# A four-layer graph network on one core: how layer 1's node stage begins

## The chip, the cores and the metric

The kernel runs on one core of one Trainium2 chip. The metric is the device time of one execution, in microseconds. The five engines of the core are called TensorE (PE in the profile; its weight loads are PEld), VectorE (DVE), ScalarE (ACT), GpSimd (POOL) and SyncE (SP); each has an instruction queue of its own and works through it in order. SyncE is used only to issue DMA transfers.

## The reference

There are 4096 nodes with 512 features in `x`, and 65536 edges. Four layers each compute `x = x + layer(relu(layernorm(x)))`. What matters here is the end of layer 0 and the beginning of layer 1:

- Layer 0 is an attention over the graph with 8 heads of 64 features. For each node and head it sums weighted rows of the neighbours, divides by the sum of the weights of that head, puts the heads side by side to a row of 512, and takes a softmax over the 512 values. `x1 = x + softmax(row)`.
- Layer 1 is a graph convolution. With `h = relu(layernorm(x1))` and `d = 1/sqrt(degree)`, a node's result is `relu(d * sum over neighbours of (d * h) @ weight)`. The kernel applies the weight first: `y = d * (h @ weight)` for all nodes, and then sums rows of `y` along the edges.
- Layer 2 (messages by a small network on each edge) and layer 3 (again a convolution) follow; nothing of them is touched.

## The kernel before

The 4096 nodes are 32 blocks of 128, one node per partition. `acc` is a tile in SBUF with one row of 522 values per node: 512 sums, 8 sums of weights (one for each head), and the node's degree. It lives through the whole kernel.

Layer 0's node part and its sorting of edges come first. Then layer 0's loop (`attend`, called through `in_two` at L816) runs over 544 tiles of 128 edges in groups of 8: GpSimd issues indirect DMAs that gather rows of `htab` (L453), ScalarE and VectorE make the weights, TensorE multiplies with one-hot matrices (L761), and VectorE adds the sums to `acc` (L768). In this loop SyncE issues nothing. The order of its instructions is written out by hand (`manual_schedule`).

Then comes the stage that this document is about, the beginning of layer 1 (L857 to L887). Here no order is written out: the framework's planner orders the instructions of each engine by its own estimate of when their inputs are ready, with the program's order as priority, so that instructions of later blocks stand between those of earlier ones. The stage works as follows.

- It loads the weight `w_sb` (1 MB) through `load_w` (L432), makes `dis`, the `1/sqrt(degree)` of all nodes, with `rsqrt` (L396 to L401: a logarithm and an exponential on ScalarE, then one Newton step of four VectorE instructions), and `rden`, the reciprocals of all the sums of weights (L862).
- It then takes the blocks in eight groups of four (`BG = 4`). For a group it loads four blocks of `x` (L865, 1 MB) into `xt`, which has two buffers.
- For each block of the group: multiply the 512 sums by the 8 reciprocals, each spread over its 64 features (L870, VectorE); row maximum (L872); its negative (L873); exponential with the row's sum (L875, ScalarE); reciprocal of that sum (L876); multiply and add to `xt` (L877).
- The group's `xt` is stored to `x1` (L878). `Norm` then makes mean and variance of each of its rows (L390, L391) and the reciprocal standard deviations of all four blocks together: add epsilon (L413) and `rsqrt`.
- For each block again: normalize into `hn` (L418), transpose it on TensorE (L425, four 128x128 pieces), ReLU into SBUF on ScalarE (L427), multiply with `w_sb` (L442; eight TensorE instructions for a block), scale by `dis` on ScalarE (L886), and store to `ytab` in HBM (L887).

Layer 1's loop over the edges (`sum_edges`) gathers rows of `ytab` by indirect DMAs on GpSimd's queue (L453), so its first gather needs all 32 blocks of `ytab`.

Two more places are named in the prediction. L448 makes one-hot matrices on VectorE; one of layer 1's loop is placed early, between instructions of this stage. And the end of layer 2 has additions on GpSimd (L1266 and L1287, 128x1024 values each) while VectorE computes norms (L1227 to L1239) and scales rows (L1303, L1305).

Of the kernel before, what the change touches and what calls it, by code (L numbers as in the profile page):

```python
# [10 lines left out]
F32 = mybir.dt.float32  # L11
# [6 lines left out]
PSUM = bass.MemoryType.PSUM  # L18
DRAM = bass.MemoryType.DRAM

P = 128
# [13 lines left out]
def kernel(  # L35
# [23 lines left out]
    nc = tc.nc  # L59
    N, D = x.shape  # L60
    E, DE = edge_attr.shape
    H, _, F = w0.shape
    KC = D // P
    NB = N // P
# [52 lines left out]
    x1 = dram.tile([N, D], F32, name="x1")  # L117
# [227 lines left out]
    class Side:  # L345


        def __init__(self, *work):
            self.work = list(work)
# [38 lines left out]
    def stats(pool, st, ap):  # L388
        six = pool.tile([P, 6], F32, name="six")
        nc.vector.bn_stats(six, ap)  # L390
        nc.vector.bn_aggr(st, six)  # L391

    def rsqrt(pool, o, ap, n):

        root = pool.tile([P, n], F32, name="root")
        nc.scalar.activation(root, ap, AF.Ln)  # L396
        nc.scalar.activation(o, root, AF.Exp, scale=-0.5)
        nc.vector.tensor_mul(root, o, o)
        nc.vector.tensor_mul(root, root, ap)
        nc.vector.tensor_scalar(root, root, -0.5, 1.5, op0=OP.mult, op1=OP.add)  # L400
        nc.vector.tensor_mul(o, o, root)  # L401

    BG = 4

    class Norm:


        def __init__(self, pool, rows):
            self.st = pool.tile([P, BG, 2], F32, name="st")
            for j, ap in enumerate(rows):  # L410
                stats(pool, self.st[:, j, :], ap)
            var = self.st[:, :, 1]
            nc.vector.tensor_scalar(var, var, EPS, None, op0=OP.add)  # L413
            self.rstd = pool.tile([P, BG], F32, name="rstd")
            rsqrt(pool, self.rstd, var, BG)

        def rows(self, j, o, ap):
            nc.vector.tensor_scalar(o, ap, self.st[:, j, 0:1], self.rstd[:, j:j + 1],  # L418
# [2 lines left out]
    def relu_t(pool, ppool, hn, relu=True):  # L421

        ps = ppool.tile([P, KC, P], F32, name="tr")
        for k in range(KC):
            nc.tensor.transpose(ps[:, k, :], hn[:, k * P:(k + 1) * P], ident)  # L425
        h_t = pool.tile([P, KC, P], F32, name="h_t")
        nc.scalar.activation(h_t, ps, AF.Relu if relu else AF.Copy)  # L427
        return h_t

    def load_w(pool, name, ap):  # L430
        t = pool.tile([P, ap.shape[0] // P, D], F32, name=name)
        nc.sync.dma_start(t, ap.rearrange("(k p) d -> p k d", p=P))  # L432
        return t
# [6 lines left out]
    def product(ps, h_t, w_sb, k0=0, start=True, stop=True):  # L440
        for k in range(KC):
            nc.tensor.matmul(ps, h_t[:, k, :], w_sb[:, k0 + k, :],  # L442
                             start=start and k == 0, stop=stop and k == KC - 1)
# [21 lines left out]
    def in_two(o, main, total, run):  # L465

        run(0, main)
        with tc.If(nc.values_load(more[:, o:o + 1], min_val=0, max_val=1) > 0):
            run(main, total)

    def blocks_of(ap, b, n=BG):
        return ap[b * P:(b + n) * P].rearrange("(b p) d -> p b d", p=P)
# [340 lines left out]

    one2 = node_pool.tile([P, 2], F32, name="one2")
    nc.vector.memset(one2, 1.0)
    in_two(0, TS_MAIN, TS, attend)  # L816
    l0_pool.close()

# [35 lines left out]
        return run  # L854

    ytab = dram.tile([N, D], F32, name="ytab")
    with tc.tile_pool(name="l1_w", bufs=1) as wp, tc.tile_pool(name="l1", bufs=2) as lp, \  # L857
            tc.tile_pool(name="l1_ps", bufs=2, space=PSUM) as lps:
        w_sb = load_w(wp, "w_sb", w_l1)
        rsqrt(lp, dis, acc[:, :, D + H], NB)  # L860
        rden = wp.tile([P, NB, H], F32, name="rden")
        nc.vector.reciprocal(rden, acc[:, :, D:D + H])  # L862
        for b0 in range(0, NB, BG):
            xt = lp.tile([P, BG, D], F32, name="xt")
            nc.sync.dma_start(xt, blocks_of(x, b0))  # L865
            for j in range(BG):
                b = b0 + j
                row = acc[:, b, :D]
                o = row.rearrange("p (h f) -> p h f", h=H)
                nc.vector.tensor_mul(o, o, rden[:, b, :].unsqueeze(2).to_broadcast([P, H, F]))  # L870
                top = lp.tile([P, 1], F32, name="top")
                nc.vector.reduce_max(top, row, axis=AX.X)  # L872
                nc.vector.tensor_scalar(top, top, -1.0, None, op0=OP.mult)  # L873
                whole = lp.tile([P, 1], F32, name="whole")
                nc.scalar.activation(row, row, AF.Exp, bias=top, accum_out=whole)  # L875
                nc.vector.reciprocal(whole, whole)  # L876
                nc.vector.scalar_tensor_tensor(xt[:, j, :], row, whole, xt[:, j, :], op0=OP.mult, op1=OP.add)  # L877
            nc.sync.dma_start(blocks_of(x1, b0), xt)  # L878
            norm = Norm(lp, [xt[:, j, :] for j in range(BG)])
            for j in range(BG):  # L880
                b = b0 + j
                hn = lp.tile([P, D], F32, name="hn")
                norm.rows(j, hn, xt[:, j, :])
                ps = lps.tile([P, D], F32, name="y_ps")
                product(ps, relu_t(lp, lps, hn), w_sb)
                nc.scalar.activation(acc[:, b, :D], ps, AF.Copy, scale=dis[:, b:b + 1])  # L886
                nc.sync.dma_start(ytab[b * P:(b + 1) * P, :], acc[:, b, :D])  # L887
# [132 lines left out]
    with ExitStack() as l2:  # L1020
        l2.enter_context(ahead)
        wp = l2.enter_context(tc.tile_pool(name="l2_w", bufs=1))
# [170 lines left out]
    with ExitStack() as end:  # L1193
        R = 2
        own = dict(reuse_waits="tile")
        wp = end.enter_context(tc.tile_pool(name="l2_end_w", bufs=1, **own))
        lp = end.enter_context(tc.tile_pool(name="l2_end", bufs=2, **own))
        lps = end.enter_context(tc.tile_pool(name="l2_end_ps", bufs=2, space=PSUM, **own))
# [60 lines left out]
        for p in range(groups + 4):  # L1259
# [22 lines left out]
            if now(p - 2):  # L1282
                b0 = (p - 2) * R
# [12 lines left out]
            if now(p - 2):  # L1296
                b0 = (p - 2) * R
                y = acc[:, b0:b0 + R, :D]
                xt = xs.pop(p - 2)
                norm = Norm2(y)  # L1300
# [8 lines left out]
                norm = Norm2(xt)  # L1309
# [3 lines left out]
            if now(p - 4):  # L1313
                b0 = (p - 4) * R
# [94 lines left out]
```

## Time and profile before

| | |
|---|---|
| median of 2 timed runs | 5975.68 us (5975.33 to 5976.02) |
| profiled execution, its own time | 6542.29 us |
| profiled execution, span from first to last instruction | 6540.2 us |
| mean granted TensorE clock, profiled | 0.926 |
| last sum of layer 0's loop (L768) | begins 1269.0 us, lasts 0.70 |
| first transpose of this stage (L425) | 1291.9 us |
| last scaling of this stage (L886) | begins 1433.1 us, lasts 0.69 |
| first gather of layer 1's loop (L453) | 1437.5 us |

The profiled execution is longer than the timed ones, so a sum of durations from it is set against its own time.

A line of the timeline gives the start in us, the duration in us (for several merged instructions from the first's start to the last's end), the engine, the line of the kernel, the operation, output `<-` inputs, the shape, how many instructions are merged, and in brackets the idle time of the engine before it and what ended that. "Issue" there means that the engine waited for nothing that the profile shows. A line of the stage table gives, for one stretch of time, the busy time and the number of instructions of each engine, the granted TensorE clock, the mean busy share of the 16 DMA engines, and the GB/s they moved. L-numbers are lines of the kernel before.

### The profile page before, as it was taken

The page shows a single profiled execution, that of the slowest core. Times are in us where ns is not written, and L with a number is a line of the kernel's source. Part 1 is how long each engine was busy: PE and PEld are TensorE (multiplying, and loading weights), DVE is VectorE, ACT ScalarE, POOL GpSimd, SP SyncE. Part 2 cuts the span into 40 slices and gives each one's busy share as a digit, 9 for nine tenths or more (in the row PEclk, how much of TensorE's full clock was granted, in tenths as well). Part 3 has the DMA queues.
Part 4 walks back from the last instruction along what each step waited for, and adds up shares of the span by engine and source line. Part 5 has one row for each costly group of instructions (what it writes and reads, how often), then busy time and mean ns, then how long its engine had stood idle before and what let it go on. Part 6 is the DMA issues. An engine that isn't in the chain of part 4 may idle for free. (4 is left out here: it accounts for less than half of the span.)

```text
span 6540.2 us, 65028 instructions
## 1 busy us (share of the span) xinstructions
PE 5567.4 (85%) x17918; PEld 2951.3 (45%) x17918; DVE 4364.9 (67%) x7420; ACT 3086.2 (47%) x4232; POOL 3919.6 (60%) x3326
## 2 busy tenths in 40 slices
PE   6576777688998869999999999999999899777777
PEld 4355555533443334444444444444444566422222
DVE  7466666755665448888888888888888555455555
ACT  3144444431110047777777777777777433100000
POOL 1255555316665658888888888888887111255664
PEclk9788888899999989999999999999999999877878
DMA  8655555456777745555555555555555111355665
GB/s 228 160 151 149 146 152 153 131 179 211 226 226 197 214 106 115 108 108 108 108 110 109 107 107 108 108 108 109 110 108 104 68 68 65 111 163 165 194 197 161
DMA packets 424659, 908.43 MB, mean 139 GB/s; under 512 B 135734, under 2 KB 135734, under 8 KB 424278
## 3 DMA queue, kind: packets, MB, share of 16 engines
q0 software_dynamic: 264768, 721.66, 44.6%
q1 hardware_dynamic: 159510, 182.40, 8.7%
q8 instruction: 153, 2.51, 0.2%
q14 instruction: 228, 1.87, 0.1%
HBM read 800.88 MB, written 102.94 MB: 138 GB/s over the span
## 5 line engine op out<-in xcount | busy, mean ns | idle before, releaser
L442 PE MATMUL m_ps<-w_sb,h_t 128*128 128x512 f32 x4224 | 1894.1, 596 | 3.2 <-ACT h_t L1081 3.0
L847 PE MATMUL sum_ps<-g,oh 128*128 128x512 f32 x2144 | 1152.5, 673 | 286.5 <-DVE acc L463 145.6
L442 PEld LDWEIGHTS m_ps<-w_sb,h_t 128*128 128x128 f32 x4224 | 781.9, 190 | 937.8 <-issue 922.9
L463 DVE TENSOR_TENSOR acc<-acc,sum_ps 128x512 f32 x800 | 550.0, 687 | 796.7 <-PE sum_ps L847 336.2
L1048 POOL DMA_INDIRECT pg<-qtab,eg x528 | 947.1, 1794 | 161.2 <-issue 160.6
L453 POOL DMA_INDIRECT pg<-ptab,eg x528 | 773.8, 1466 | 217.3 <-issue 160.3
L761 PE MATMUL sum_ps<-rows,oh 128*128 128x261 f32 x2176 | 619.3, 440 | 287.5 <-issue 197.6
L847 PEld LDWEIGHTS sum_ps<-g,oh 128*128 128x128 f32 x2144 | 429.1, 212 | 951.4 <-issue 574.1
L453 POOL DMA_INDIRECT g<-ytab,s_dst x544 | 544.7, 1001 | 491.3 <-DMA x_mid<-x 201.0
L453 POOL DMA_INDIRECT rows<-htab,s_dst x544 | 518.1, 952 | 482.1 <-PE sum_ps L761 285.6
L453 POOL DMA_INDIRECT g<-ztab,d_src x528 | 511.6, 969 | 409.5 <-PE sum_ps L847 173.2
L761 PEld LDWEIGHTS sum_ps<-rows,oh 128*128 128x128 f32 x2176 | 453.5, 217 | 391.8 <-issue 203.8
L988 POOL DMA_INDIRECT eg<-aug,d_eid x528 | 517.6, 980 | 160.9 <-issue 142.9
L1081 ACT COPY h_t<-tr_ps 128x512 f32<-128x512 f32 x528 | 296.3, 587 | 292.5 <-PE tr_ps L1079 271.7
L1349 ACT ACTIVATE t_end<-acc,dis 128x512 f32<-128x512 f32 x32 | 23.0, 722 | 847.9 <-DVE acc L463 806.4
L463 DVE TENSOR_TENSOR acc<-acc,small_ps 128x512 f32 x528 | 362.5, 687 | 80.2 <-DVE acc L463 60.6
L1099 PE MATMUL small_ps<-parts,oh 128*128 128x512 f32 x1056 | 314.9, 420 | 91.4 <-DVE parts L1093 80.7
L1156 DVE TENSOR_TENSOR pg<-pg,small_ps 128x512 f32<-128x512 f32 x528 | 328.3, 683 | 66.3 <-issue 38.6
L1152 DVE TENSOR_TENSOR z<-m_ps,b_bc 128x512 f32<-128x512 f32 x132 | 91.3, 692 | 376.7 <-PE m_ps L442 345.8
L1093 DVE TENSOR_TENSOR parts<-z,parts 128x1024 fp32r<-128x1024 f32 x264 | 323.4, 1225 | 9.0
L1079 PE MATMUL tr_ps<-ident,pg 128*128 128x128 f32 x2112 | 302.3, 276 | 5.4 <-DVE pg L1167 2.1
L768 DVE TENSOR_TENSOR acc<-acc,sum_ps 128x522 f32 x272 | 189.5, 697 | 173.7 <-PE sum_ps L761 159.6
(276 smaller groups left out, 8716.9 us busy)
## 6 DMA issues: line engine op xcount, KB each, us to landing
aug<-row SPq DMA_DIRECT2D x32, 560.0 KB
xt<-in_x_dram SPq DMA_DIRECT2D x16, 1024.0 KB
row<-in_edge_attr_dram SPq DMA_DIRECT2D x32, 512.0 KB
rows<-htab,s_dst POOLq DMA_INDIRECT x544
g<-ytab,s_dst POOLq DMA_INDIRECT x544
eg<-aug,d_eid POOLq DMA_INDIRECT x528
pg<-ptab,eg POOLq DMA_INDIRECT x528
pg<-qtab,eg POOLq DMA_INDIRECT x528
```

Of the source, the lines that this page charges most:

```text
L442: nc.tensor.matmul(ps, h_t[:, k, :], w_sb[:, k0 + k, :], start=start and k == 0, stop=stop and k == KC - 1)
L453: nc.gpsimd.indirect_dma_start(out=dst_ap, out_offset=None, in_=table, in_offset=bass.IndirectOffsetOnAxis(ap=idx, axis=0))
L463: nc.vector.tensor_add(into, into, ps)
L761: nc.tensor.matmul(ps[:, c, :HW], oh[:, j + k, :], rows[:, j + k, c * HW:(c + 1) * HW], start=k == 0, stop=k == 1)
L847: nc.tensor.matmul(ps, oh[:, j + k, :], g[:, j + k, :], start=k == 0, stop=k == pair - 1)
L988: nc.gpsimd.indirect_dma_start(out=eg[:, j // 2, (j % 2) * HALF:(j % 2 + 1) * HALF], out_offset=None, in_=aug.rearrange("e c -> (e c)").un ...
L1048: nc.gpsimd.indirect_dma_start(out=pg[:, j, :], out_offset=None, in_=qtab, in_offset=bass.IndirectOffsetOnAxis(ap=end_of(eg, j, 1), axis=0 ...
L1079: nc.tensor.transpose(h_ps[:, k, :], h[:, j, k * P:(k + 1) * P], ident)
L1081: nc.scalar.copy(h_t, h_ps)
L1093: nc.vector.tensor_sub(parts[:, 1], m, parts[:, 0].bitcast(F32))
L1099: nc.tensor.matmul(ps, oh, parts[:, k], start=k == 0, stop=k == 1)
L1156: nc.vector.tensor_add(nxt[:, j], nxt[:, j], made[j])
```

## The change

The change has four parts.

1. `w_sb` and the first four blocks of `x` (`x_first`, 1 MB) are fetched ahead of layer 0's loop, into a pool `l1_first` on the other side of SBUF that stays open until the stage ends.
2. The first four blocks are worked on in groups of 1, 1 and 2, out of `x_first`; from block 4 on the groups are of four as before. `Norm` and `rsqrt` take the number of blocks of the group.
3. `xt` has three buffers instead of two.
4. The products of the sums with the reciprocals (L870) stay on VectorE for blocks 0 and 1, and are made by GpSimd for blocks 2 to 31.

```diff
     def rsqrt(pool, o, ap, n):
-        root = pool.tile([P, n], F32, name="root")
+        root = pool.tile([P, n], F32, name=f"root{n}")
...
         def __init__(self, pool, rows):
             self.st = pool.tile([P, BG, 2], F32, name="st")
+            n = len(rows)
             for j, ap in enumerate(rows):
                 stats(pool, self.st[:, j, :], ap)
-            var = self.st[:, :, 1]
+            var = self.st[:, :n, 1]
             nc.vector.tensor_scalar(var, var, EPS, None, op0=OP.add)
             self.rstd = pool.tile([P, BG], F32, name="rstd")
-            rsqrt(pool, self.rstd, var, BG)
+            rsqrt(pool, self.rstd[:, :n], var, n)
...
     nc.vector.memset(one2, 1.0)
+
+    l1_first = ExitStack()
+    wp = l1_first.enter_context(tc.tile_pool(name="l1_w", bufs=1, side="right"))
+    w_sb = load_w(wp, "w_sb", w_l1)
+    x_first = wp.tile([P, BG, D], F32, name="x_first")
+    nc.sync.dma_start(x_first, blocks_of(x, 0))
     in_two(0, TS_MAIN, TS, attend)
...
-    with tc.tile_pool(name="l1_w", bufs=1) as wp, tc.tile_pool(name="l1", bufs=2) as lp, \
-            tc.tile_pool(name="l1_ps", bufs=2, space=PSUM) as lps:
-        w_sb = load_w(wp, "w_sb", w_l1)
+    with l1_first, tc.tile_pool(name="l1", bufs=2) as lp, tc.tile_pool(name="l1_ps", bufs=2, space=PSUM) as lps:
         rsqrt(lp, dis, acc[:, :, D + H], NB)
         rden = wp.tile([P, NB, H], F32, name="rden")
         nc.vector.reciprocal(rden, acc[:, :, D:D + H])
-        for b0 in range(0, NB, BG):
-            xt = lp.tile([P, BG, D], F32, name="xt")
-            nc.sync.dma_start(xt, blocks_of(x, b0))
-            for j in range(BG):
+
+        for b0, n in [(0, 1), (1, 1), (2, 2)] + [(b, BG) for b in range(BG, NB, BG)]:
+            xt = x_first[:, b0:b0 + n] if b0 < BG else lp.tile([P, BG, D], F32, name="xt", bufs=3)
+            if b0 >= BG:
+                nc.sync.dma_start(xt, blocks_of(x, b0))
+            for j in range(n):
                 b = b0 + j
                 row = acc[:, b, :D]
                 o = row.rearrange("p (h f) -> p h f", h=H)
-                nc.vector.tensor_mul(o, o, rden[:, b, :].unsqueeze(2).to_broadcast([P, H, F]))
+                (nc.vector if b < 2 else nc.gpsimd).tensor_mul(o, o, rden[:, b, :].unsqueeze(2).to_broadcast([P, H, F]))
...
-            nc.sync.dma_start(blocks_of(x1, b0), xt)
-            norm = Norm(lp, [xt[:, j, :] for j in range(BG)])
-            for j in range(BG):
+            nc.sync.dma_start(blocks_of(x1, b0, n), xt)
+            norm = Norm(lp, [xt[:, j, :] for j in range(n)])
+            for j in range(n):
```

## The prediction

> **What bounds the kernel now.** I read the page for the whole, then the stage table of layer 1's beginning, the groups of that stretch, and its timeline. The page shows one core with TensorE busy 85% of a span of 6540.2 us, but no stage of 6540 us is touched here: the change sits between the last sum of layer 0's loop (1269 us) and the first gather of layer 1's loop (1437.5 us).
>
> ```profile
> core 0: us, PE busy (x) PEld busy (x) DVE busy (x) ACT busy (x) POOL busy (x), PEclk, DMA share, GB/s
> 1269.00:1292.00 23.00, 0.08 (x1) 0.11 (x2) 19.71 (x55) 6.17 (x18) 0.00 (x0) 0.60 0.51 184
> 1292.00:1434.00 142.00, 130.91 (x384) 63.62 (x384) 88.36 (x251) 57.73 (x129) 0.00 (x0) 0.98 0.43 154
> ```
>
> Read two regimes: 23 us in which TensorE does nothing and VectorE is busy for 19.7, then 142 us in which TensorE is busy and VectorE has slack. GpSimd does nothing in either. Within the second, the timeline repeats this every two blocks:
>
> ```profile
> 1416.12 1.04 PE L425 MATMUL tr<-ident,hn 128*128 128x128 f32 x8
> 1417.55 7.13 PE L442 MATMUL y_ps<-w_sb,h_t 128*128 128x512 f32 x16 [0.39 <-ACT h_t L427]
> 1424.52 1.04 PE L425 MATMUL tr<-ident,hn 128*128 128x128 f32 x8
> ```
>
> 1424.52 - 1416.12 = 8.40 us for two blocks, 4.2 per block. 32 blocks are 134.4; from the first transpose (1291.92) to the last product's end (1433.1) are 141.2. The rest is the slow clock of the first products and some waits. So the end of the stage is the start of TensorE plus a constant, as long as VectorE delivers `hn` in time. What holds the start:
>
> ```profile
> 1270.65 2.41 SPq L865 DMA_DIRECT2D xt<-in_x_dram  x2
> 1272.98 1.75 DVE L862 RECIPROCAL rden<-acc 128x256 f32<-128x256 f32 x1 [3.29 <-issue]
> ...
> 1278.17 0.72 ACT L875 ACTIVATE acc<-acc,top 128x512 f32<-128x512 f32 x1 [7.50 <-DVE top L873]
> ...
> 1281.29 1.41 DVE L877 SCALAR_TENSOR_TENSOR xt<-acc,whole,xt 128x512 f32<-128x512 f32 x2
> ...
> 1287.95 0.17 DVE L413 TENSOR_SCALAR st<-st 128x4 f32<-128x4 f32 x1
> ...
> 1291.08 0.99 DVE L418 TENSOR_SCALAR hn<-xt,st,rstd 128x512 f32<-128x512 f32 x2
> ```
>
> VectorE works through four blocks before the first `hn`. `xt` came from memory in time: L877 has no idle time before it.
>
> [...] The trace agrees, in layer 2's end, where GpSimd adds 128x1024 tiles:
>
> ```profile
> 5315.99 2.36 POOL L1266 TENSOR_TENSOR h_sb<-h_sb,b_bc 128x1024 f32<-128x1024 f32 x1 [26.90 <-PE tr L1250]
> 5318.30 2.35 POOL L1287 TENSOR_TENSOR xs<-xs,beta_bc 128x1024 f32<-128x1024 f32 x1
> ```
> ```profile
> 5316.39 1.98 DVE L1227 TENSOR_SCALAR st<-st 128x2 f32<-128x2 f32 x1
> 5318.40 2.27 DVE L1230 TENSOR_SCALAR down<-st 128x2 f32<-128x2 f32 x1
> 5320.59 0.16 DVE L1233 TENSOR_SCALAR half<-st 128x2 int32<-128x2 int32 x1
> 5190.70 2.65 DVE L1305 SCALAR_TENSOR_TENSOR xs<-acc,rstd,xs 128x512 f32<-128x512 f32 x1
> 5193.28 2.84 DVE L1303 SCALAR_TENSOR_TENSOR acc<-acc,st,gamma_bc 128x512 f32<-128x512 f32 x1
> ```
>
> An instruction of 0.17 us lasts 1.98: it ends with the GpSimd one (5318.35), and the next GpSimd one starts at once and catches the next small VectorE one for 2.27. The 0.75 us instructions with two tensor inputs last 2.65 and 2.84. So they alternate, and each VectorE instruction of these kinds waits out one GpSimd instruction. That is what decides this change for me.
>
> **The change part by part.**
>
> *Fetches moved into layer 0's loop.* Two issues of SyncE (`w_sb` and `x_first`, 1 MB each) move ahead of the loop, past nothing on SyncE's queue, which has no transfer in the loop. They save no wait on the path, since L877 did not wait for x and TensorE started 20 us after `w_sb` was issued. The cost: they go out near 271 us, when the first gathers start (276.0 to 285.8, waited for until 289.0). 2 MB at the 304 GB/s of 1270 to 1280 us are 6.9 us of DMA. The gathers leave a quarter idle (share 0.74 to 0.75). If the fetches run from 271.5, 3.9 us of their work is left at 276, and up to 288.7 the gathers need 9.5 of 12.7 us: 0.7 us late. If they start only behind the small-row transfer to `htab`, up to 3.8 late. Below nothing is excluded: nobody in the loop uses them. I take 0.5.
>
> *`xt` in three buffers.* VectorE waited 15.1 us for `xt` in four waits, but behind a TensorE that had work. The cover is the queue of finished `hn`; taken at 0, a gain of up to 2.
>
> *Groups of 1, 1 and 2.* Block 0's `hn` no longer waits for blocks 1 to 3. Two extra groups add two times L413 and L398 to L401, ten instructions of 0.16: 1.6 us of VectorE, four of `Ln`/`Exp` at 0.2 on ScalarE, and two stores of x1 on SyncE (0.37 each), all beside TensorE. Without any contention: up to the first `Exp` nothing changes (1278.17, ends 1279.1); reciprocal, L877, statistics, with one filling instruction of another block for each, end at about 1282.3; from L413 to the end of the first `hn` the old timeline took 3.65 (1287.95 to 1291.6), so 1286, 5.6 us earlier.
>
> *Products on GpSimd.* VectorE loses 30 times 0.683 (L870) = 20.5 us. It had slack later, so this is off the path but for the beginning. GpSimd gets 30 instructions of 128x512. Price: half of 2.35 us is 1.18; with a fixed part of 0.2 (estimate, from its 0.31 us copies of 48 elements) 1.28. [...] I take 1.2: 36 us. Nothing holds them back after `rden`: they need no buffer, and the queue holds nothing else until the gathers. So they run in a row from 1274.8[...]. VectorE's own exclusive time there (about 6 us of L870, L877, L418) makes them end near 1317.
>
> Now the chain to the first `hn`, in the order that the old timeline had. From 1274.7: the early one-hot L448 0.68; then L399, the product of block 0, L400, the product of block 1 and L401, five instructions that each wait a GpSimd one (5 x 1.2) and 0.55 for each product: 1282.5. Old: 1276.9. L872 twice and L873[...]: exp at 1284.0 to 1284.9. Reciprocal, then L877 waits 0.6 on average: 1286.4. L877 of block 1 is in front of the rest (1.75), statistics in its shadow or behind: 1288.5. Ln and Exp: 1289.0. L398, L399, L401: 0.6 + 1.2 + 1.2; L418 1.2 + 0.4: 1293.6. If one-element L400 and L413 are caught too, or two of block 1's are put between, 3.6 more: 1297.2. I take 1295.4 against 1291.6: **TensorE starts 3.8 us later, not 5.6 earlier.**
>
> TensorE then does blocks 0 and 1 at first with the slow clock. Weight loads in the old start were 0.85 us apart until 1297, then 0.43: block 0 0.97 + 0.65 + 5 x 0.85 + 3 x 0.43 = 7.2, block 1 4.4: done at 1307. Block 2's `hn` still needs two L877, L413, four of L398 to L401 and L418, eight caught instructions from 1299 on: 8 x 1.25 + 1 = 11, and one or two L877 of blocks 4 and 5 in between, 1.75 each: 1313. The old kernel began block 2 at 1302.2. From there it needed 130.9 to the end; at 4.2 per block 126, so it lost 4.9 to waits. With VectorE at 3.1 per block (3.8 less 0.7) I give back 2, and block 4, whose group must be whole by 1321.6, takes 1 to 2 of it again. **Sum: 10.8 later + 0.5 - 1 = about +10 us** at the stage's end. Layer 1's loop needs all of ytab, so it passes this on whole; its own start is the same.
>
> On the profiled execution: 6542.29 + 10 = 6552. The timed runs, without a profile, have a median of 5975.68, 8.7% less; in this stage the clock was full and no indirect DMA ran, so I carry the 10 us over unscaled: **5985.7**.
>
> Bounds: contention of the wide instructions alone with products of 1.1 us: +3; products of 1.28 us with every small instruction caught and block 4 waiting 5 us: +20. Measurements tell apart about 2% (119 us); nothing here comes near that.
>
> **Rivals.** (a) *Contention bites little; the new order wins.* It holds if the scheduler puts GpSimd's products or VectorE's small instructions so that they rarely meet, or if L398 to L401 at one element aren't caught. Then the start is 5.6 earlier and up to 2.5 of the old waits go: 5975.7 - 8 = 5968. For: 23 us of idle TensorE are there to be had. Against: the two caught instructions above. It decides if fewer than five of the some fourteen chain instructions are caught. (b) *They cancel*: some seven are caught, and the faster VectorE makes up the rest: 5976, within 4. (c) *The fetches hit the loop's start* at the 3.8 us bound on top of the contention at its upper bound: 5975.7 + 20 + 3.8 = 5999. (d) *The loads do not move*: if their memory were taken until the loop ends, they would wait as before; times as in the first case, since nothing on the path waited for them.
>
> **How the numbers follow.** Contention, +5 to +20 (with d in it): 0.55. Rival (a), -4 to -10: 0.25. Rival (b): 0.15. Rival (c) or worse: 0.05. Range 5966 to 5996; the likeliest case alone 5980 to 5996. Over 2% either way has no case of its own: 0.01 and 0.02.
>
> **What would show it.** Right: 30 GpSimd products of 1.2 us from 1275 without pause; L398 to L401 and L877 means in that stretch near 1.2 and 1.7 instead of 0.16 and 0.75; first transpose at 1294 to 1298; TensorE idle again ahead of block 2; the first gather near 1447. Wrong: first transpose before 1289 with small VectorE instructions of 0.16 us, or the first sum of layer 0's loop moved by more than 4 us.

## The result, and the profile after

The changed kernel takes 5980.68 us (median of 2 runs, 5980.40 to 5980.97) against 5975.68 us before: 5.0 us more, a ratio of 1.0007 with a 95% interval of 0.9983 to 1.0031. That interval reaches from 10 us less to 19 us more, so by time alone there is no difference; by the profile there is one, in the stage that was changed.

L-numbers of the changed kernel differ from those of the kernel before: L867 makes the reciprocals of the sums, L877 is the products with them (L870 before), L879 and L880 the row maximum and its negative, L882 the exponential, L883 the reciprocal of the row's sum, L884 the addition to x (L877 before), L414 adds epsilon, L419 normalizes, L426 transposes, L428 copies the transposed row into SBUF, L443 multiplies with the weight and L893 scales by `dis`. L396 to L401 are the roots as before, L449 the early one-hot matrix.

Three stretches of the changed kernel, in the same table as before. The last sum of layer 0's loop begins at 975.5 us here.

```profile
core 0: us, PE busy (x) PEld busy (x) DVE busy (x) ACT busy (x) POOL busy (x), PEclk, DMA share, GB/s
976.00:1002.00 26.00, 1.09 (x4) 0.72 (x4) 23.33 (x47) 5.48 (x17) 21.29 (x18) 0.56 0.42 148
1002.00:1016.00 14.00, 9.93 (x20) 4.46 (x21) 14.00 (x25) 4.49 (x12) 14.00 (x13) 0.74 0.13 47
1016.00:1147.00 131.00, 121.88 (x361) 58.70 (x359) 70.64 (x214) 55.16 (x122) 0.90 (x1) 1.00 0.41 149
```

The idle start of TensorE was 23 us. Now there are 26 us with one set of four transposes in them, and then 14 us in which TensorE is busy for 9.9 and VectorE and GpSimd for all 14. Only when GpSimd is done does TensorE run through.

From here on a stage is measured from the start of the loop's last sum to the start of the stage's last scaling by `dis` (before: L886). It was 164.1 us (1433.1 - 1269.0), and 162.6 in a second profile of the kernel before; it is now 170.5 (1146.0 - 975.5), and 171.8 in a second profile of the changed kernel. Two profiles of one kernel thus differ by 1.3 to 1.5 us, and smaller differences show nothing. The first gather of layer 1's loop follows 4.2 us behind the stage here, 4.4 and 4.8 before. The stage has lost 6.3 to 9.2 us. Differences are taken before rounding.

GpSimd's and VectorE's groups between 976 and 1016 us, by shape (group, shape and count | busy us, mean ns | idle before):

```profile
L877 POOL TENSOR_TENSOR acc<-acc,rden 128x512 f32<-128x512 f32 x30 | 36.2, 1243 | 20.2 <-DVE root L398 20.2
...
L884 DVE SCALAR_TENSOR_TENSOR xt<-acc,whole,xt 128x512 f32<-128x512 f32 x4 | 6.3, 1566 | 0.0
...
L398 DVE TENSOR_TENSOR root<-rstd 128x1 f32<-128x1 f32 x2 | 2.0, 990 | 0.0
...
L399 DVE TENSOR_TENSOR root<-root,acc 128x32 f32<-128x32 f32 x1 | 1.1, 1052 | 0.0
L400 DVE TENSOR_SCALAR root<-root 128x32 f32<-128x32 f32 x1 | 1.0, 1015 | 0.0
L400 DVE TENSOR_SCALAR root<-root 128x2 f32<-128x2 f32 x1 | 1.0, 999 | 0.0
...
L400 DVE TENSOR_SCALAR root<-root 128x1 f32<-128x1 f32 x2 | 0.3, 142 | 0.0
```

I call an instruction caught when it lasts longer than alone while GpSimd makes a product. Caught ones of 0.13 to 0.21 us take up to 1.05; the four L884 shown here, 0.74 us alone, take 1.52 to 1.61. Not every one is caught: of the first four L884, those on `x_first`, three take 0.74 to 0.81. One kind is spared in this stretch: `tensor_scalar` on a single element per partition, 0.14 us. Then ScalarE's timeline in the changed kernel, around the first copies of transposed rows:

```profile
1000.88 0.72 ACT L882 ACTIVATE acc<-acc,top 128x512 f32<-128x512 f32 x1 [4.81 <-DVE top L880]
1001.51 0.19 ACT L882 ACTIVATION_READ_ACCUMULATOR acc<-acc,top 128x1 f32 x1
1001.60 0.58 ACT L428 ACTIVATE h_t<-tr 128x512 f32<-128x512 f32 x1
...
1010.87 0.72 ACT L882 ACTIVATE acc<-acc,top 128x512 f32<-128x512 f32 x1 [3.63 <-DVE top L880]
1011.50 0.19 ACT L882 ACTIVATION_READ_ACCUMULATOR acc<-acc,top 128x1 f32 x1
1011.60 0.67 ACT L893 ACTIVATE acc<-y_ps,dis 128x512 f32<-128x512 f32 x1
1012.17 1.10 ACT L428 ACTIVATE h_t<-tr 128x512 f32<-128x512 f32 x2
```

And TensorE's in the same stretch:

```profile
997.42 1.09 PE L426 MATMUL tr<-ident,hn 128*128 128x128 f32 x4 [21.96 <-DVE hn L419]
1002.28 5.64 PE L443 MATMUL y_ps<-w_sb,h_t 128*128 128x512 f32 x8 [3.76 <-POOL acc L877]
1007.75 0.60 PE L426 MATMUL tr<-ident,hn 128*128 128x128 f32 x4
1011.97 0.66 PE L426 MATMUL tr<-ident,hn 128*128 128x128 f32 x4 [3.62 <-DVE hn L419]
1012.80 8.83 PE L443 MATMUL y_ps<-w_sb,h_t 128*128 128x512 f32 x16 [0.17 <-ACT h_t L428]
...
1023.58 3.70 PE L443 MATMUL y_ps<-w_sb,h_t 128*128 128x512 f32 x8 [1.51 <-ACT h_t L428]
```

The row that block 2's transposes wait for, from VectorE's timeline:

```profile
1010.76 1.16 DVE L419 TENSOR_SCALAR hn<-x_first,st,rstd 128x512 f32<-128x512 f32 x1
```

The transposes of block 0 end at 998.51, but ScalarE copies them only at 1001.60, since an exponential of a later block stands ahead in its queue and waits 4.81 us for a maximum from VectorE. The 3.76 us that the trace puts down to GpSimd are this wait. Block 1: ready at 1008.35, copied at 1012.17, behind an exponential that waited 3.63 and a scaling.

These two late copies are not what holds the stage. In TensorE's queue block 2's transposes stand ahead of block 1's products, and they wait 3.62 us for block 2's row from VectorE; behind them the products wait only 0.17 us for block 1's copy. VectorE works without a pause from its reciprocals at 978.87 until that row is done at 1011.92, and beyond. With the instructions in this order, earlier copies would only have made TensorE wait longer for the row. ScalarE does hold TensorE at block 3: its products wait 1.51 us for the copy, and 3.22 in the second profile, and begin 48.1 us after the last sum in both. Before they began 38.6 and 37.4 us after it, so there TensorE is 9.5 to 10.7 us behind. In the first profile about 3 us of that are won back up to the end, where TensorE waits less from there on (2.2 us in waits of over 0.5 us, against 6.7 in the first profile before).

Behind the wait of 3.62 us TensorE's granted clock, 0.99 from 1006.2 to 1008.4 us, is 0.63 from 1012.0 to 1016.2.

### The profile page after: what moved, and what is told of

Its sections match the earlier page's. It is cut to its first block, busy times and chain, and to the rows that moved or that the text cites. A ratio compares the mean times of both kernels' runs of the same rounds, so it can differ in the third digit from the quotient of the medians.

```text
span 5979.2 us, 65067 instructions
## 1 busy us (share of the span) xinstructions
PE 5358.1 (90%) x17918; PEld 2809.6 (47%) x17918; DVE 4360.0 (73%) x7400; ACT 3085.6 (52%) x4236; POOL 3959.3 (66%) x3356
## 5 line engine op out<-in xcount | busy, mean ns | idle before, releaser
L443 PE MATMUL m_ps<-w_sb,h_t 128*128 128x512 f32 x4224 | 1893.9, 596 | 3.2 <-ACT h_t L1088 3.2
L443 PEld LDWEIGHTS m_ps<-w_sb,h_t 128*128 128x128 f32 x4224 | 781.9, 190 | 937.1 <-issue 922.2
L854 PE MATMUL sum_ps<-g,oh 128*128 128x512 f32 x2144 | 1073.9, 618 | 157.7 <-DMA g<-ztab,d_src 92.3
L854 PEld LDWEIGHTS sum_ps<-g,oh 128*128 128x128 f32 x2144 | 378.1, 192 | 792.3 <-issue 335.7
L762 PE MATMUL sum_ps<-rows,oh 128*128 128x261 f32 x2176 | 528.0, 390 | 113.8 <-issue 105.9
L762 PEld LDWEIGHTS sum_ps<-rows,oh 128*128 128x128 f32 x2176 | 398.6, 191 | 196.4 <-issue 131.5
L1273 POOL TENSOR_TENSOR h_sb<-h_sb,b_bc 128x1024 f32<-128x1024 f32 x16 | 37.9, 2371 | 444.9 <-PE tr L1257 358.1
```

What stands on the lines that cost most here:

```text
L443: nc.tensor.matmul(ps, h_t[:, k, :], w_sb[:, k0 + k, :], start=start and k == 0, stop=stop and k == KC - 1)
L762: nc.tensor.matmul(ps[:, c, :HW], oh[:, j + k, :], rows[:, j + k, c * HW:(c + 1) * HW], start=k == 0, stop=k == 1)
L854: nc.tensor.matmul(ps, oh[:, j + k, :], g[:, j + k, :], start=k == 0, stop=k == pair - 1)
```

## The experiments

The theory: GpSimd's products hold up VectorE's instructions, as its additions in layer 2's end do in the profile before (1.98 us for 0.17, 2.65 and 2.84 for 0.75), so VectorE's short chains at the start of the stage stretch. Rival 1: the small groups themselves cost the time. Rival 2: waiting for GpSimd's results costs it, not GpSimd's presence. Rival 3: the early fetches cost something in layer 0's loop.

Three chips were used: one for the second profile of the kernel before, all products on VectorE, GpSimd's products alone and idle products; one for half of the products, late fetches, small groups and the first run of the reciprocals in pieces; one for idle writes and the second runs of the changed kernel and of the reciprocals in pieces. On the second and third the loops over edges take longer for every kernel, as they do in the first profile of the kernel before: layer 0's last sum begins at 1252 to 1272 us there, and at 975 to 985 in the other profiles. So each ratio is against the kernel before on the same chip, while stage lengths are compared across chips. The ratios are as recorded; quotients of the medians that the text gives differ from them by up to 0.001, 6 us, and their intervals reach about as far to either side. So the stage lengths carry the argument, and the times must agree with them.

| kernel | first transpose, us after the last sum | stage, us | ratio to before (95%) |
|---|---|---|---|
| before, two profiles | 22.9, 22.7 | 164.1, 162.6 | 1 |
| changed, two profiles on different chips | 21.9, 21.9 | 170.5, 171.8 | 1.0007 (0.9983 to 1.0031), 1.0007 (0.9995 to 1.0019) |
| all products on VectorE | 17.0 | 156.1 | 0.9993 (0.9986 to 0.9999) |
| GpSimd's products alone | 34.8 | 178.5 | 1.0023 (1.0014 to 1.0033) |
| idle products on GpSimd | 22.7 | 168.5 | 1.0014 (1.0007 to 1.0020) |
| idle writes on GpSimd | 17.2 | 156.0 | 0.9988 (0.9976 to 1.0001) |
| half of the products on GpSimd | 24.0 | 165.6 | 0.9999 (0.9986 to 1.0013) |
| changed, late fetches | 26.0 | 175.6 | 1.0008 (0.9993 to 1.0023) |
| small groups alone | 19.0 | 156.9 | 0.9979 (0.9969 to 0.9989) |
| reciprocals in pieces, two runs | 14.9, 14.7 | 153.7, 153.4 | 0.9982 (0.9967 to 0.9997), 0.9976 (0.9965 to 0.9988) |

**The kernel before, once more**

> The kernel before, unchanged, for a second profile: layer 0's loop ended at 1269 us in the first one and at 976 in the changed kernel's, so the first is no base for anything outside the stage. Both theories: 5975.7 us; the loop's end near 976 us; from the start of the loop's last sum to the start of the stage's last scaling 164.1 us as in the first profile (1433.1 - 1269.0), and 22.9 us to the first transpose. If the stage itself comes out 170 here, the 6 us that I put down to the change are the profile's.

5979.85 us, the same as the runs of the kernel before beside it (ratio 1.0, 0.9991 to 1.0009). The loop's last sum begins at 979.3, the stage takes 162.6. So the first profile's 164.1 stands, and the loss of the stage is the change's; only the long loop was particular to that profile.

**All products on VectorE**

```diff
-                (nc.vector if b < 2 else nc.gpsimd).tensor_mul(o, o, rden[:, b, :].unsqueeze(2).to_broadcast([P, H, F]))
+                nc.vector.tensor_mul(o, o, rden[:, b, :].unsqueeze(2).to_broadcast([P, H, F]))
```

> The changed kernel with all products back on VectorE; early fetches, groups of 1, 1, 2 and three buffers stay. [...] the stage from the loop's last sum to the last scaling falls from 170.4 to 157 to 160 us, the first transpose comes 17 us after that sum instead of 21.9, the small instructions of the reciprocal roots take 0.16 us, and the time is 5967 to 5970, 11 to 14 less than the changed kernel. Rival, the small groups themselves cost it (more small instructions, ScalarE's exponentials queued ahead of the copies for TensorE): the stage stays at 168 to 171 us, the time at 5979 to 5982.

The first transpose comes at 17.0, as the theory had it; the stage, 156.1, is 0.9 us under the expected range. Time 5976.69 against 5981.17 before (0.9993), a smaller gain than in the stage. The rest of the change is worth 6.5 to 8.0 us in the stage; the products on GpSimd turn that into a loss of about the same size. Its groups of VectorE in the same stage (970 to 1300 us):

```profile
L884 DVE SCALAR_TENSOR_TENSOR xt<-acc,whole,xt 128x512 f32<-128x512 f32 x28 | 20.6, 739 | 0.0
...
L398 DVE TENSOR_TENSOR root<-rstd 128x1 f32<-128x1 f32 x2 | 0.3, 152 | 0.0
...
L399 DVE TENSOR_TENSOR root<-root,acc 128x32 f32<-128x32 f32 x1 | 0.2, 206 | 0.0
L400 DVE TENSOR_SCALAR root<-root 128x32 f32<-128x32 f32 x1 | 0.2, 175 | 0.0
...
L400 DVE TENSOR_SCALAR root<-root 128x2 f32<-128x2 f32 x1 | 0.2, 159 | 0.0
```

And its TensorE timeline, where the waits ahead of the products are 0.73 and 0.61 us:

```profile
1001.55 1.08 PE L426 MATMUL tr<-ident,hn 128*128 128x128 f32 x4 [17.03 <-DVE root L399]
1003.37 6.31 PE L443 MATMUL y_ps<-w_sb,h_t 128*128 128x512 f32 x8 [0.73 <-issue]
1009.52 0.82 PE L426 MATMUL tr<-ident,hn 128*128 128x128 f32 x6
1010.95 3.70 PE L443 MATMUL y_ps<-w_sb,h_t 128*128 128x512 f32 x8 [0.61 <-ACT h_t L428]
```

The granted clock is 1.00 from 1010.9 to 1015.0 here; the 8 products from 1010.95 take 3.70 us, as the 8 from 1023.58 do in the changed kernel, where the clock is 1.00 from 1023 to 1028.

**GpSimd's products alone**

```diff
-                nc.vector.tensor_mul(o, o, rden[:, b, :].unsqueeze(2).to_broadcast([P, H, F]))
+                (nc.vector if b < 2 else nc.gpsimd).tensor_mul(o, o, rden[:, b, :].unsqueeze(2).to_broadcast([P, H, F]))
```
(in the kernel before)

> The kernel before with one edit: products of blocks 2 to 31 on GpSimd; groups of four, late fetches, two buffers. [...] the first transpose 30 to 36 us after the loop's last sum (22.9 before), since the four blocks' small and two-input instructions are all caught ahead of it; stage 170 to 176 us; time 5982 to 5988. Rival, the groups are what costs: VectorE has 20 us less to do, the first transpose comes at 20 to 22 us, the stage takes 161 to 164, the time is 5973 to 5976.

With groups of four, more caught instructions stand ahead of the first row. TensorE's timeline:

```profile
1017.74 2.15 PE L425 MATMUL tr<-ident,hn 128*128 128x128 f32 x8 [34.83 <-DVE hn L418]
```

34.8 us instead of 22.9, stage 178.5, beyond the expected 170 to 176; 5995.55 us against 5981.17, beyond the expected 5982 to 5988 and slower clear of noise. Giving VectorE 20 us less to do made the stage 14 to 16 us longer. The groups aren't the cost (rival 1 falls): together with the early fetches and the third buffer they soften it, from 178.5 to 170.5.

**Idle products on GpSimd**

All products on VectorE, and GpSimd makes 30 that nobody uses.

```diff
+        junk = wp.tile([P, D], F32, name="junk_pool")
...
                 nc.vector.tensor_mul(o, o, rden[:, b, :].unsqueeze(2).to_broadcast([P, H, F]))
+                if b >= 2:
+                    nc.gpsimd.tensor_mul(junk.rearrange("p (h f) -> p h f", h=H),
+                                         w_sb[:, 0, :].rearrange("p (h f) -> p h f", h=H),
+                                         rden[:, b, :].unsqueeze(2).to_broadcast([P, H, F]))
```

> As the run with all products on VectorE, and beside that GpSimd makes 30 products of the same shape that nobody uses (a row of the weight times the same reciprocals, into a tile of their own), so GpSimd is as busy as in the changed kernel but nothing waits for its results. [...] being there is enough, VectorE is caught just so and has 30 products more: stage 171 to 180 us, time 5982 to 5991. Rival, it is the waiting for GpSimd's results, 1.24 us each instead of 0.68 on VectorE, that delays the rows: as the run with all products on VectorE without them, stage 157 to 160, time 5967 to 5970.

Stage 168.5 and not 156.1: 12.4 of the 14.3 us that separate the changed kernel from the one without GpSimd's products come with nobody waiting for a result. On this one chip the time says the same, 5988.67 us against 5976.69, 12.0 more. I had expected a stage of 171 to 180, longer than the changed kernel's since VectorE has 20 us more to do; it is 2 us shorter. Where these 2 us come from is open. In the changed kernel VectorE has no idle time from 978.87 to beyond block 2's row, so up to there it waited for no result. Its groups (970 to 1300 us):

```profile
L419 DVE TENSOR_SCALAR hn<-x_first,st,rstd 128x512 f32<-128x512 f32 x4 | 4.6, 1160 | 0.0
...
L398 DVE TENSOR_TENSOR root<-rstd 128x1 f32<-128x1 f32 x2 | 2.0, 994 | 0.0
...
L399 DVE TENSOR_TENSOR root<-root,acc 128x32 f32<-128x32 f32 x1 | 1.1, 1055 | 0.0
L400 DVE TENSOR_SCALAR root<-root 128x32 f32<-128x32 f32 x1 | 1.0, 1014 | 0.0
```

Rival 2 falls but for at most those 2 us.

**Idle writes on GpSimd**

The idle products replaced, for each of the 30 blocks, by

```diff
+                    nc.gpsimd.tensor_copy(junk[:, :H], rden[:, b, :])
+                    for _ in range(2):
+                        nc.gpsimd.memset(junk, 0.0)
```

> As the run with idle products on GpSimd, but GpSimd mostly writes: for each of blocks 2 to 31 one copy of 8 reciprocals and two fills of a 128x512 tile with zero, results that nobody uses; all products on VectorE. If a VectorE instruction with two inputs is held up only by a GpSimd instruction that reads SBUF, L398, L399, L401 and L884 keep their 0.15 and 0.75 us[...]: first transpose 17 to 19 us after the loop's last sum, stage 156 to 160 us. [...]

The 60 fills took 0.54 us each, so GpSimd was busy for 32.4 us with them; the small copies, which do read, took 0.29 each. Stage 156.0, first transpose at 17.2: as if GpSimd did nothing. Had any work of GpSimd held VectorE up, I expected 166 to 169 and 22 to 23, as with the idle products. The groups (1250 to 1292 us), where L889 is the addition to x:

```profile
L889 DVE SCALAR_TENSOR_TENSOR x_first<-acc,whole,x_first 128x512 f32<-128x512 f32 x4 | 3.0, 740 | 0.0
L419 DVE TENSOR_SCALAR hn<-x_first,st,rstd 128x512 f32<-128x512 f32 x4 | 2.8, 711 | 0.5 <-PE tr L426 0.5
...
L414 DVE TENSOR_SCALAR st<-st 128x2 f32<-128x2 f32 x1 | 0.6, 608 | 0.0
...
L399 DVE TENSOR_TENSOR root<-root,acc 128x32 f32<-128x32 f32 x1 | 0.2, 207 | 0.0
```

Instructions with two tensor inputs keep their 0.74 and 0.2 us; `tensor_scalar` on 512 elements takes 0.71 for 0.54, and L414 on 2 elements 0.61 for 0.17. So it is not GpSimd's being busy that makes the loss in this stage: fills, which read no tensor, leave it at 156.0 us, and products, which read two, make it 168.5. That their reading does it fits both runs, but products and fills differ in operation and length as well, so this was not shown by itself.

**Half of the products on GpSimd**

```diff
-                (nc.vector if b < 2 else nc.gpsimd).tensor_mul(o, o, rden[:, b, :].unsqueeze(2).to_broadcast([P, H, F]))
+                (nc.vector if b < 17 else nc.gpsimd).tensor_mul(o, o, rden[:, b, :].unsqueeze(2).to_broadcast([P, H, F]))
```

> The changed kernel with GpSimd making only the products of blocks 17 to 31, VectorE those of blocks 0 to 16: 15 GpSimd instructions in a row instead of 30, some 18 to 21 us from the end of the reciprocals. [...] they still cover the whole chain to the first transpose, which comes 21 to 23 us after the loop's last sum as in the changed kernel, and then VectorE is free: stage 162 to 166 us, between 156.1 (none) and 170.5 (30); time 5 to 8 us less than the changed kernel's, so 0 to 3 us over the kernel before. Rival, what costs is that ScalarE and VectorE wait for GpSimd's late results: the blocks that these products serve come 60 us later, nobody waits, and the stage is 156 to 158.

Stage 165.6. The results of blocks 17 to 31 are needed much later, yet their 15 products run in a row at the start (19.4 us), and the first transpose comes at 24.0, even later than with 30 and than the expected 21 to 23; why it is later is not shown. After that VectorE is free, and 4.8 to 6.2 us come back. The wait for results can't explain this run at all.

**Late fetches**

```diff
-    l1_first = ExitStack()
-    wp = l1_first.enter_context(tc.tile_pool(name="l1_w", bufs=1, side="right"))
-    w_sb = load_w(wp, "w_sb", w_l1)
-    x_first = wp.tile([P, BG, D], F32, name="x_first")
-    nc.sync.dma_start(x_first, blocks_of(x, 0))
...
-    with l1_first, tc.tile_pool(name="l1", bufs=2) as lp, tc.tile_pool(name="l1_ps", bufs=2, space=PSUM) as lps:
+    with tc.tile_pool(name="l1_w", bufs=1) as wp, tc.tile_pool(name="l1", bufs=2) as lp, \
+            tc.tile_pool(name="l1_ps", bufs=2, space=PSUM) as lps:
+        w_sb = load_w(wp, "w_sb", w_l1)
+        x_first = wp.tile([P, BG, D], F32, name="x_first")
+        nc.sync.dma_start(x_first, blocks_of(x, 0))
```

> The changed kernel with its weight and the first four blocks of x fetched where the kernel before fetches them, after layer 0's loop; groups, buffers and GpSimd's products stay. Theory: the fetches are off the path both ways. The rows are needed 13.8 us after the loop's last sum in the changed kernel and 2 MB land some 9 to 10 us after it; the weight is needed after 26. Stage 169.5 to 171.5 us, time as the changed kernel's, 5 to 8 us over the kernel before. Rival, the early fetches delay layer 0's loop and are part of the loss: 1 to 4 us less than the changed kernel.

Stage 175.6, 3.8 to 5.1 more than the changed kernel's. My expectation was wrong; the fetches aren't off the path. But not because data came late. Its VectorE timeline around the additions to x (L883 here):

```profile
1276.73 0.15 DVE L879 TENSOR_SCALAR top<-top 128x1 f32<-128x1 f32 x1
1276.80 2.76 DVE L883 SCALAR_TENSOR_TENSOR x_first<-acc,whole,x_first 128x512 f32<-128x512 f32 x2
...
1287.96 0.67 DVE L419 TENSOR_SCALAR hn<-x_first,st,rstd 128x512 f32<-128x512 f32 x1
```

The additions begin 13.9 us after the last sum with no idle time in front, as in the changed kernel (13.8). What differs is the planner's order: blocks 0 and 1 are now added as a pair, block 0's statistics and roots stand behind, and the first row is normalized 25.1 us after the last sum instead of 21.0. That the planner does so because it expects x later is my reading, not shown. VectorE waits for no transfer in this stretch. It does wait 3.33 us for an exponential later on, at 48 us, which it doesn't in the changed kernel, and TensorE waits 4.03 us for block 2's row, where it waited 3.62.

Rival 3: from the first to the last sum of layer 0's loop there are 679.2 us in the kernel before and 680.7 with GpSimd's products alone, both with late fetches, and 682.2 and 680.2 with all products on VectorE and with idle products, both with early ones, all on one chip. That is 1.3 us more on average, with 1.5 to 2.0 between equals; no delay is shown.

**Small groups alone**

The kernel before with groups of 1, 1 and 2 and three buffers: the late fetches of the previous diff, and all products on VectorE.

> The kernel before with groups of 1, 1, 2 and three buffers alone: late fetches, all products on VectorE. The row of x is now needed 10.4 us after the loop's last sum, about when the fetch lands. Theory: the groups alone bring the gain; stage 156 to 159 us, time 3 to 7 us under the kernel before. Rival, the early fetch is what makes the small groups pay: the first transpose comes at 19 to 22 us instead of 16.9, stage 159 to 162, time 0 to 3 us under.

First transpose at 19.0, where the rival had it, but stage 156.9, where the theory had it. The groups with the third buffer bring 5.7 to 7.2 us; what the third buffer does alone was not measured. With the early fetch beside them (all products on VectorE) the first transpose comes 2.0 us earlier, but the stage is only 0.8 shorter, less than two profiles of one kernel differ, so without GpSimd's products no gain from the fetch is shown. The median is 8.6 us under the kernel before on its chip, its ratio clear of 1.

**Reciprocals in pieces**

All products on VectorE, with

```diff
-        rsqrt(lp, dis, acc[:, :, D + H], NB)
         rden = wp.tile([P, NB, H], F32, name="rden")
-        nc.vector.reciprocal(rden, acc[:, :, D:D + H])
+        nc.vector.reciprocal(rden[:, :2], acc[:, :2, D:D + H])
...
                 o = row.rearrange("p (h f) -> p h f", h=H)
+                if b >= 2 and j == 0:
+                    nc.vector.reciprocal(rden[:, b0:b0 + n], acc[:, b0:b0 + n, D:D + H])
...
                 norm.rows(j, hn, xt[:, j, :])
+                if b == 0:
+                    rsqrt(lp, dis, acc[:, :, D + H], NB)
```

> All products on VectorE, early fetches and small groups, and in addition the reciprocals of the sums of weights are taken in pieces, those of blocks 0 and 1 first (0.2 us instead of 1.75 ahead of the first product), and the degree's roots are asked for after the first rows. Theory: the chain to the first transpose loses 1.5 to 2.3 us: 14.6 to 15.5 us after the loop's last sum, stage 153.5 to 155 us, time 1 to 3 us under the run with all products on VectorE and 5 to 9 under the kernel before. Rival, TensorE waits later for block 2 whatever the start: stage 156.

Stage 153.7, first transpose at 14.9, median 6.4 us under the kernel before, all as the theory had it. To have it beside the changed kernel on one chip, both ran again:

> The changed kernel unchanged, beside the two others of this call, so that the three stand on one chip. Theory: stage from the loop's last sum to the last scaling 170 to 171 us on whatever chip, 5 to 8 us over the kernel before in time. If the stage is 174 to 176 as with the late fetches, those 5 us came from the chip and not from the fetches; if it is 170.5, the fetches are worth 5 us beside GpSimd's products, and my step that put them off the path is wrong.

> The version with all products on VectorE and the reciprocals in pieces once more, now on one chip with the changed kernel: stage 153.5 to 154.5 us, 16 to 17 us under the changed kernel in stage and time, and 8 to 12 us under the kernel before.

The changed kernel's stage is 171.8 here, near its first 170.5, so the 3.8 to 5.1 us of the late fetches stand. Its time is no difference again: the median, 6529.13 us, is 1.6 under the kernel before's 6530.75, while the recorded ratio is 1.0007, with 1 inside its interval. The expected 5 to 8 us more are not seen in time. The version with pieces: stage 153.4, 6512.54 us. It beats the changed kernel by 16.6 us (18.3 in the stage) and the kernel before by 18.2, a ratio clear of 1; expected were 8 to 12, and 9.2 to 10.7 are seen in the stage. The rest lies within the interval. Its VectorE and TensorE timelines at the start:

```profile
1262.15 0.25 DVE L866 RECIPROCAL rden<-acc 128x16 f32<-128x16 f32 x1 [2.69 <-issue]
1262.32 0.20 DVE L877 RECIPROCAL rden<-acc 128x16 f32<-128x16 f32 x1
1262.44 0.69 DVE L878 TENSOR_TENSOR acc<-acc,rden 128x512 f32<-128x512 f32 x1
...
1267.32 0.74 DVE L885 SCALAR_TENSOR_TENSOR x_first<-acc,whole,x_first 128x512 f32<-128x512 f32 x1
```
```profile
1273.45 1.09 PE L426 MATMUL tr<-ident,hn 128*128 128x128 f32 x4 [14.73 <-DVE root L399]
1275.28 5.86 PE L443 MATMUL y_ps<-w_sb,h_t 128*128 128x512 f32 x8 [0.73 <-issue]
1280.97 1.04 PE L426 MATMUL tr<-ident,hn 128*128 128x128 f32 x8
```

The first product starts 0.3 us after the first reciprocal; with all products on VectorE and one reciprocal for all it was 2.4 (987.99 to 990.42). How much of the gain comes from the pieces and how much from the later roots is not separated. TensorE waits 0.73 us between its first transposes and products, as with all products on VectorE, where it waited 3.76 in the changed kernel.

## Why the prediction was right, and where it was off

**The time** agrees with the forecast (5985.7, measured 5980.68), but there is luck in it. The interval of the measured ratio also allows for no change, and the kernel before would lie in the forecast range of 5966 to 5996 as well. What bears the forecast out is the mechanism, in the profiles.

**The bound** was read rightly. In steady state two blocks take 8.40 us after as before (1120.55 to 1128.95), and what TensorE has lost by block 3 shows at the end but for 1.5 to 3.2 us.

**The contention** was the right cause. Forecast were 30 GpSimd products in a row from 1274.8 at 1.2 us, that is 5.8 us after the loop's last sum; they came 5.2 us after it, with 36.18 us for 30, 1.21 each. One alone takes 1.04, and up to 1.57 when it waits for VectorE itself; the 1.18 that the forecast took as half of 2.35 lies between. Caught small instructions take 1.0 us, forecast near 1.2. The idle products (168.5 us) show that no result need be waited for, the idle writes (156.0) that a busy GpSimd alone is not enough.

**The chain to the first row** was oversized. The step said that TensorE starts 3.8 us later; it starts 1.0 us earlier (21.9 for 22.9). Without GpSimd's products it starts at 17.0, which the uncontended 1286 (17.0) had right. So the contention on this chain is 4.9 us and not 9.4. The trace has two reasons. First, a caught instruction ends 0.01 to 0.07 us behind the product under way, and a product that isn't held up itself takes 1.04 us, within which lie the instruction's own 0.15 to 0.2; so being caught costs about 0.85 us (L399: 1.05 for 0.21) and not 1.2. Second, of the chain only five were caught for 0.8 us or more: L399, L400 and L401 of the degree's roots, one L877, and one L398. L449 was caught for 0.64 and the others for under 0.3. Reductions and statistics, which aren't held up (L879 0.67 us and L390 0.68, as with all products on VectorE), stand in between. One-element L400 and L414 were never caught (0.14 and 0.13 us), while L400 on two elements took 1.0; why one element is spared is not shown.

**Behind the start** the forecast was VectorE's lateness, with TensorE idle ahead of block 2, and that came: it idles 3.62 us there for VectorE's row. The row itself was oversized like the first, forecast at 44 us after the last sum and begun at 35.3. From the first transpose to the last scaling the forecast had 6 us more than before (10.8 less 3.8, less 1); measured are 148.5 us against 141.2 and 139.9, 7.3 to 8.6 more. So the lateness weighs about as forecast, though the row is earlier. The forecast lacked that block 1's products stand behind block 2's transposes, so that block 2's products begin only at 42.5, against 35.1 and 33.8 before. It also lacked the wait for ScalarE's copy at block 3.

**The sum** of +10 at the stage's end measured +6.3 in the first profiles and up to +9.2 over both of each kernel. The mis-sized term is the start (3.8 later, measured 1.0 earlier), made up in part by the larger loss behind it. Two of the named signs did not come: the first transpose was to be 25 to 29 us after the last sum (21.9), and the first gather 178 (174.7).

**The fetches** at the loop's start, 0.5 us, can't be seen: the loop's first sum begins at 295.0 us, against 295.7 and 300.2 before. The lower bound in that step is off by its own numbers: 6.9 us of DMA less the 4.5 from 271.5 to 276 leave 2.4 and not 3.9, and the 3.2 us that the gathers leave would have held them. That the fetches gain nothing was wrong: beside GpSimd's products they are worth 3.8 to 5.1 us, with another order from the planner and no wait for data. I had asked only who waits for the data. They were also issued before the loop's gathers, at 261.6 us (the weight, in the sorting stage) and 265.9, and not near 271.

**The rivals.** That contention bites little and the new order wins is not what came, though the order is worth 6.5 to 8.0 us, forecast 8, once GpSimd is out of it. The line was drawn at five caught instructions of the chain, and five were. That they cancel can't be told from the time (5.0 more, with an interval wider than that), but the stage loses 6.3 us or more. The fetches at their bound, 5999 us, lie outside the interval, which ends at 5994. That the loads do not move is excluded; both went out before the loop.

## What to carry to other kernels

In this stage moving an elementwise product to an idle GpSimd wasn't free: VectorE's instructions with two tensor inputs, and `tensor_scalar` on two or more elements, waited for it, the smallest ones most in proportion (1.05 us for 0.21 and 1.00 for 0.16, against 1.57 for 0.74). It harmed where a chain of small VectorE instructions starts the stage and GpSimd's work is ready all at once; half of the products made the start as late as all (24.0 us against 21.9). And where a planner orders the engines, follow each queue behind the stretched engine as well, and ask of each late instruction whether something else is later still. Here ScalarE's queue, worked through in order, passed VectorE's delay to copies that were ready (ready at 998.51, made at 1001.60 behind an exponential that waited 4.81 us); for blocks 0 and 1 TensorE waited longer for VectorE anyway, for block 3 it waited for the copy.

## What I had not expected of the hardware

- A caught small VectorE instruction costs 0.85 us beside products of 1.04 to 1.57, not a whole product, and one-element `tensor_scalar` in the roots is never caught (0.13 to 0.15 us in every run that has it).
- GpSimd that mostly writes (fills of 128x512, 0.54 us each, 32.4 us in all) leaves instructions with two tensor inputs at 0.74 us and the stage at 156.0 us.
- In the changed kernel a wait of TensorE of 3.62 us behind its first products goes with a granted clock of 0.63 in the 4.2 us from its end on, 0.99 ahead of it. With all products on VectorE, where the waits there are 0.73 and 0.61 us, the clock is 1.00 in the 4.1 us behind the second.
- The same kernel takes 5981 us on one chip and 6531 to 6535 on two others. Between 300 and 970 us the granted TensorE clock is 0.99 and the DMA share 0.76 in a profile from the first, 0.85 and 0.53 in one from another, while this stage takes the same time within about 1.5 us. Which comes first, the slower gathers or the lower clock, is left open.
